# Two attention layers on one core: bias sums of the second projection at other steps and in other banks, the first biases split ahead of v, and products of constants in the prologue

## The chip, the core and the metric

The kernel runs on one core of one Trainium2 chip. The metric is the time of one execution on the device, in microseconds (us). All inputs, weights and results are float32 and lie in the device's memory; they are laid out on the host beforehand.

## The reference

The input x has shape 4 x 32 x 32 x 768 (4 images of 1024 tokens). Two attention layers follow each other, each as x = x + layer(group_norm(x)). Cut to what matters:

```python
# layer 0
q, k, v = heads(xn @ Wq + bq), heads(xn @ Wk + bk), heads(xn @ Wv + bv)   # 12 heads of 64
attn = q @ k.T / 8 + rel_bias_h(q)[..., None] + rel_bias_w(q)[..., None, :]
x = x + softmax(attn) @ v @ Wp + bp
# layer 1
q, k, v = split(xn @ w_qkv.T + b_qkv)
q, k, v = [layer_norm(dwconv3x3(t, w_pool)) * g + b for t in (q, k, v)]
attn = (q * scale) @ k.T + rel_h(q)[..., None] + rel_w(q)[..., None, :]
o = softmax(attn) @ v + q
x = x + o @ w_proj.T + b_proj
```

## The kernel before

**Stages, pairs and steps.** A stage is one image in one layer; there are eight, in the order (image 0, layer 0), (1, 0), (0, 1), (1, 1), (2, 0), (3, 0), (2, 1), (3, 1). Each stage has six pairs of heads, so there are 48 pairs. The attention of a pair (`attend`, L687) is written as 16 steps: two chunks of 512 queries, two groups of four key tiles for each chunk, and four steps for each group. A group issues the scores of its four key tiles (lines L748 and L750: the product of q and k, and the biases added by a second product), the exponentials on ACT (L755) and the running sums on DVE (L762, L764), then has two steps in which other work is put in, then issues the weighted sums (`av`, L770), then again has two steps for other work. Other work is put in by step number through `at(step, piece)` and the table `events`; steps below 0 make the prologue.

**Order.** The order on PE, DVE, ACT and POOL is the program's order (a manual schedule), so an instruction that waits holds up all that follows on its engine. SP, whose queue starts the loads and stores, is not in that list: its order is decided by the compiler's scheduler.

**PSUM banks.** The scores use a fixed pair of banks for the first and the fourth key tile and two places, `place_b` and `place_c`, for the second and the third. Between the scores those places serve the other work: `bank(name)` hands out the next of a list that is set anew after the scores and after `av` (`behind_av` is place_c, place_c, the small bank, place_b, place_b). `small_bank(name)` is a single bank of its own. It is also used by the means of the group norm (`gn_mean` L322, `gn_var` L331), by the softmax's sums (`z`, L712) and by some products of layer 0.

**Bias.** The relative positions of a pair are computed by `positions` (L575): small products `rel` into PSUM, copied by ACT into the tile `whole` (L595, L596). `split` (L601) rounds `whole` into `high` on ACT (L606), leaves the rest in `whole` on DVE (L607), and spreads both over the tile `bias` by eight DMAs on POOL's queue for each chunk of queries (L617). The bias products L750 read that tile. `plan` (L620) lists for each pair which piece stands at which of its steps; the first two pairs use the first list, in which the products of v (`plain_v`) come in two halves. Pair 0's pieces stand at steps -16 to -6, that is, in the prologue.

**Sums of weights.** Products are done in a form with seven products for eight, which needs sums of blocks of the weights. `mix_weights(u)` (L263) loads two blocks (`mix_a`, `mix_b`), yields, then forms five sums on DVE (L291) and stores them (L292). For layer 1's projection (u of 12, 13 and 14) it first multiplies the unmixed weights by the v norm's offset: six products of one column for each block, L281, into a `pbias` bank, which DVE adds to the projection's bias (L282). A table of (u, call, step) says at which step the loads are called and at which the sums are formed.

**Prologue.** `group_norm` of the first stage ends with `gn_mean`, `gn_var`, a few operations of one column on DVE and ACT (`rsqrt`), and six operations that normalize xn (L338). The products of q and k of pair 0 (`qkv`, issued by the helper `halves`, L131) wait for these. `halves` issues each product as two halves of 64 output columns.

Of the kernel before, what the change touches and what calls it, by code (L numbers as in the profile page):

```python
# [17 lines left out]
P = 128  # L18
# [27 lines left out]
def two_layers(ctx: ExitStack, tc: tile.TileContext, keep, x_in, wqkv, wproj, rels, windows, vrow, small, const, onehot, picks, out):  # L46
# [19 lines left out]
    nc = tc.nc  # L66
# [52 lines left out]
    def bank(name):  # L119

        place = turn.pop(0)
        turn.append(place)
        return place.single(name) if place else small_bank(name)

    def small_bank(name):
        return ps_small.tile([P, 512], F32, tag="small", name=name)
# [14 lines left out]
    cst = fixed.tile([P, NCONST], F32, tag="cst", name="cst")  # L141
    nc.sync.dma_start(cst, const)
    ident = cst[:, IDENT : IDENT + P]
# [6 lines left out]
    def rsqrt(v, n, name):  # L150

        ln = stat.tile([P, n], F32, tag=f"ln{n}", name=f"ln_{name}")
        nc.scalar.activation(ln, v, AF.Ln)
        r = stat.tile([P, n], F32, tag=f"r{n}", name=f"r_{name}")
        nc.scalar.activation(r, ln, AF.Exp, scale=-0.5)
        t = stat.tile([P, n], F32, tag=f"t{n}", name=f"t_{name}")
        nc.vector.tensor_mul(t, r, r)
        nc.vector.tensor_mul(t, t, v)
        nc.vector.tensor_scalar(t, t, -0.5, 1.5, ALU.mult, ALU.add)
        nc.vector.tensor_mul(r, r, t)  # L160
        return r


    stages = [(b0 + k, layer) for b0 in range(0, B, 2) for layer in range(2) for k in range(2)]
# [98 lines left out]
    def mix_weights(u):  # L263


        a = wp.tile([P, NC, P], F32, tag="wproj", name="mix_a")
        b = wp.tile([P, NC, P], F32, tag="wproj", name="mix_b")
        if u < PROJ_SUMS:
            (pa, sa), (pb, sb) = two(u, 0) if u < V_SUMS else two(2 * (u - V_SUMS), 2)
            nc.sync.dma_start(a, wqkv[0, pa, :, sa])  # L270
            nc.sync.dma_start(b, wqkv[0, pb, :, sb])
        else:
            layer, m = divmod(2 * (u - PROJ_SUMS), NC)
            for i, w in enumerate((a, b)):
                nc.sync.dma_start(w, wproj[layer, :, :, m + i, :].rearrange("h p q -> p h q"))
        yield
        for i, w in enumerate((a, b)):
            if u >= PROJ_SUMS and layer:
                ps = small_bank("pbias")
                for n in range(NC):  # L280
                    nc.tensor.matmul(ps[:, 0:1], w[:, n, :], col(LN + 5), start=(n == 0), stop=(n == NC - 1))  # L281
                nc.vector.tensor_tensor(pbias[:, m + i : m + i + 1], ps[:, 0:1], col(BIAS[1] + 18 + m + i), ALU.add)  # L282
        a1, a2, b1, b2 = a[:, :3, :], a[:, 3:, :], b[:, :3, :], b[:, 3:, :]
        for n, to, x, y, op in (
            (2, None, a1, b2, ALU.add), (4, None, b1, a1, ALU.subtract), (0, b1, b1, b2, ALU.add),
            (1, a1, a1, a2, ALU.add), (3, a2, a2, b2, ALU.subtract),
        ):
            if to is None:
                to = wp.tile([P, HALF], F32, tag="x", name="mix")
                to = to[:, : 3 * P].rearrange("p (n c) -> p n c", c=P)  # L290
            nc.vector.tensor_tensor(to, x, y, op)  # L291
            nc.sync.dma_start(mixed[u][:, n], to)  # L292
        mixed_there.add(u)
        yield
# [12 lines left out]
    def group_norm(stage):  # L307

        xn = xns[stage]
        st = stat.tile([P, NC * 2, 6], F32, tag="bn", name="bn", bufs=1)  # L310
        for n in range(NC):
            for h in range(2):
                nc.vector.bn_stats(st[:, 2 * n + h, :], xn[:, n, h * HALF : (h + 1) * HALF])
            if n in (1, 3):
                yield
        mv = stat.tile([P, 2], F32, tag="mv", name="mv")
        nc.vector.bn_aggr(mv, st.rearrange("p a b -> p (a b)"))
        yield
        yield
        group = cst[:, GROUP : GROUP + P]  # L320
        ps = small_bank("gn_mean")
        nc.tensor.matmul(ps[:, 0:1], group, mv[:, 0:1], start=True, stop=True)  # L322
        mean = stat.tile([P, 1], F32, tag="gmean", name="gmean")
        nc.vector.tensor_copy(mean, ps[:, 0:1])  # L324
        d = stat.tile([P, 1], F32, tag="gd", name="gd")
        nc.vector.tensor_sub(d, mv[:, 0:1], mean)
        nc.vector.scalar_tensor_tensor(d, d, d, mv[:, 1:2], ALU.mult, ALU.add)
        yield
        yield
        ps = small_bank("gn_var")  # L330
        nc.tensor.matmul(ps[:, 0:1], group, d, start=True, stop=True)  # L331
        v = stat.tile([P, 1], F32, tag="gv", name="gv")
        nc.vector.tensor_scalar(v, ps[:, 0:1], EPS, None, ALU.add)
        yield
        r = rsqrt(v, 1, "gn")
        yield
        for n in range(NC):
            nc.vector.tensor_scalar(xn[:, n, :], xn[:, n, :], mean, r, ALU.subtract, ALU.mult)  # L338
            if n % 2:
                yield  # L340
# [22 lines left out]
    class Pair:  # L363
# [256 lines left out]
        def plan(self):  # L620

            Q, K, V = 0, 1, 2
            if not self.layer and not in_sevens(self.i):
                return [
                    (0, lambda: self.plain(Q, 0)),
                    (2, lambda: self.plain(Q, 1)),
                    (4, lambda: self.plain(K, 0)),
                    (5, lambda: self.positions(0)),
                    (6, lambda: self.plain(K, 1)),
                    (7, lambda: self.positions(1)),  # L630
                    (8, lambda: self.plain_v(0)),
                    (10, lambda: self.split()),
                    (10, lambda: self.plain_v(1)),
                ]
            if not self.layer:
                pieces = [
                    (0, lambda: self.sevens(Q, False)),
                    (2, lambda: self.sevens(Q, True)),
                    (6, lambda: self.positions(0)),
                    (8, lambda: self.positions(1)),  # L640
                    (10, lambda: self.split()),
                ]
                if self.hp % 2 == 0:
                    pieces += [(8, lambda: self.sevens(V, False)), (10, lambda: self.sevens(V, True))]
                return [(r + shift(self.i), piece) for r, piece in pieces]

            pieces = [
                (-8, lambda: self.padded(Q, 0)),
                (-6, lambda: self.padded(Q, 1)),
                (-4, lambda: self.padded(K, 0)),  # L650
                (-2, lambda: self.padded(K, 1)),
                (2, lambda: self.padded(V, 0)),
                (4, lambda: self.padded(V, 1)),
                (3, lambda: self.centre(Q)),
                (5, lambda: self.squares(Q)),
                (7, lambda: self.norm(Q)),
                (8, lambda: self.centre(K)),
                (9, lambda: self.back(Q, 0)),
                (9, lambda: self.back(Q, 1)),
                (10, lambda: self.squares(K)),  # L660
                (10, lambda: self.positions(0)),
                (11, lambda: self.positions(1)),
                (12, lambda: self.norm(K)),
                (12, lambda: self.split()),
                (13, lambda: self.centre(V)),
                (14, lambda: self.back(K, 0)),
                (14, lambda: self.back(K, 1)),
                (14, lambda: self.squares(V)),
                (15, lambda: self.norm(V)),
            ]  # L670

            taps = (
                (Q, -4, (2, 2, 2, 2, 1)),
                (K, 2, (2, 2, 2, 2, 1)),
                (V, 8, (2, 2, 3, 2)),
            )
            for s, r, counts in taps:
                lo = 0
                for n in counts:
                    pieces.append((r, lambda s=s, lo=lo, n=n: self.taps(s, lo, lo + n)))  # L680
                    r, lo = r + 1, lo + n
            return pieces
# [233 lines left out]

    for u, call, step in (
        (2, 0, 5), (7, 6, 11), (3, 13, 18), (4, 22, 29), (8, 31, 38), (5, 40, 47), (0, 49, 55), (6, 57, 63), (1, 65, 71),
        (9, 72, 77), (10, 78, 83), (11, 84, 89), (12, 138, 143), (13, 145, 150), (14, 152, 157),
    ):  # L920
        mix = mix_weights(u)
        for at_step in (call, step):
            at(at_step, lambda mix=mix: next(mix))
# [348 lines left out]
```

## Time and profile before

| what | us |
|---|---|
| runs of the kernel before | 3919.93, 3915.82, 3917.45 |
| their median | 3917.45 |
| the profiled execution's own time | 3920.75 |
| its span, from the first to the last instruction | 3918.9 |
| PE busy | 3835.0 (98%) |
| DVE busy | 2673.5 (68%) |
| ACT busy | 1850.3 (47%) |
| mean granted clock of TensorE | 0.993 |

How to read it: 1.85 us of the profiled execution lie outside its span. PE is the matrix engine (TensorE), DVE the vector engine, ACT the scalar engine, POOL and SP start transfers here. A busy PE is not a PE at its peak: its clock can be granted at half (0.50) for a while, and a product then takes twice as long while the engine still counts as busy. PE's idle time and its time at half clock are therefore read separately, the first from the list of waits and the second from tables by stretches of time.

### The profile page before, as it was taken

To read this page: it belongs to the slowest core of one execution; us is meant where nothing else is said; L and a number is where in the kernel's file an instruction comes from. 1 tells how busy PE (TensorE), PEld (TensorE's weight loads), DVE (VectorE), ACT (ScalarE), POOL (GpSimd) and SP (SyncE) were. 2 spreads that over 40 slices of the span, in tenths; PEclk is the share of its full clock that TensorE was granted. 3 is DMA by queue.
4 is the path that set the end of the run, shared out by engine and by line. 5 is a ranking of instruction groups with operands and counts; after the bars stand their busy time and mean duration, and the time that the engine had idled before them with its cause. 6 is when DMAs were issued, how large, how long until landed. Compare 5 with 4: busy or idle time off the path is not lost.

```text
span 3918.9 us, 79880 instructions
## 1 busy us (share of the span) xinstructions
PE 3835.0 (98%) x34738; PEld 1726.2 (44%) x34738; DVE 2673.5 (68%) x3088; ACT 1850.3 (47%) x2741; POOL 411.7 (11%) x776
## 2 busy tenths in 40 slices
PE   7999999999999999999899999999999999999998
PEld 3535535534344444444444455355443444434442
DVE  2566454448789988799654554445686898878885
ACT  2455434445345553455533554254553555535551
POOL 0111000110000010000010010011100010000010
PEclk9999999999999999999999999999999999999999
DMA  4344452331331122311144222522115121142112
GB/s 147 102 120 120 127 163 61 94 83 38 105 100 39 39 60 83 115 45 39 41 118 135 56 73 64 167 63 75 42 52 155 35 56 43 39 118 57 36 47 95
DMA packets 184710, 318.11 MB, mean 81 GB/s; under 512 B 24352, under 2 KB 77472, under 8 KB 184352
## 3 DMA queue, kind: packets, MB, share of 16 engines
q1 hardware_dynamic: 122912, 212.19, 17.3%
q0 software_dynamic: 61440, 100.71, 11.2%
q8 instruction: 277, 4.54, 0.5%
q14 instruction: 81, 0.66, 0.1%
HBM read 172.23 MB, written 39.91 MB: 54 GB/s over the span
## 4 chain that ended last, share of the span: by engine, by line
PE 86%; DVE 11%; DMA 1%; issue 1%; ACT 1%; POOL 0%; DVEq 0%; SPq 0%; ACTq 0%
PE qkv L131 18%; PE s L748 15%; PE av L770 15%; PE m4m L131 4%; PE m3m L131 4%; PE m1m L131 4%; PE s L750 4%; DVE shared L532 3%; PE p3p L131 3%; DVE acc L764 3%; PE p1p L131 3%; PE p4p L131 3%; PE ln_c L131 3%; PE rel L590 3%; PE z L712 2%; PE m L131 2%
## 5 line engine op out<-in xcount | busy, mean ns | idle before, releaser
L755 ACT ACTIVATE e<-s 128x1024 f32<-128x1024 f32 x768 | 777.2, 1025 | 412.1 <-PE s L750 379.5
L764 DVE TENSOR_TENSOR acc<-acc,e 128x1024 f32<-128x1024 f32 x576 | 705.5, 1225 | 182.7 <-ACT e L755 132.2
L131 PE MATMUL qkv<-xn,wqkv_t 128*64 128x512 f32 x3648 | 815.8, 596 | 6.8 <-DVE gmean L324 4.1
L748 PE MATMUL s<-q,k 64*128 64x512 f32 x3072 | 817.1, 609 | 4.3 <-ACT e L755 3.5
L532 DVE SCALAR_TENSOR_TENSOR shared<-shared,sm 128x1056 f32<-128x1056 f32 x576 | 758.4, 1317 | 15.0
L750 PE MATMUL s<-bias,ones 64*128 64x512 f32 x1536 | 617.0, 796 | 10.9 <-DMA bias<-high 7.5
L770 PE MATMUL av<-e,vt 128*64 128x512 f32 x2624 | 595.0, 595 | 0.0
L617 POOL DMA_DIRECT2D bias<-high x384 | 203.6, 546 | 3237.8 <-ACT high L606 3003.6
L131 PEld LDWEIGHTS qkv<-xn,wqkv_t 128*64 128x64 f32 x3648 | 254.2, 137 | 491.5 <-issue 481.6
L515 ACT ACTIVATE shared<-qkv,sm 128x512 f32<-128x512 f32 (+1 forms) x288 | 129.3, 502 | 632.7 <-PE qkv L131 632.7
L748 PEld LDWEIGHTS s<-q,k 64*128 64x128 f32 x3072 | 283.2, 188 | 263.2 <-issue 216.8
L770 PEld LDWEIGHTS av<-e,vt 128*64 128x64 f32 x2624 | 185.6, 137 | 347.1 <-issue 322.0
L762 DVE TENSOR_TENSOR acc<-e 128x1024 f32<-128x1024 f32 x96 | 117.5, 1224 | 285.9 <-ACT e L755 280.1
L750 PEld LDWEIGHTS s<-bias,ones 64*128 64x128 f32 x1536 | 150.8, 189 | 199.2 <-issue 191.6
L617 POOL DMA_DIRECT2D bias<-whole x384 | 206.1, 558 | 106.6 <-DVE whole L607 97.0
L705 ACT COPY weighed<-av 128x512 f32<-128x512 f32 x96 | 56.4, 587 | 279.3 <-PE av L770 279.3
L131 PEld LDWEIGHTS ln_c<-cst,shared 128*64 128x64 f32 x2304 | 130.9, 137 | 48.5 <-issue 41.0
L590 PEld LDWEIGHTS rel<-q,rel 64*32 64x32 f32 x6144 | 111.7, 105 | 78.0 <-issue 58.7
L131 PE MATMUL ln_c<-cst,shared 128*64 128x128 f32 x2304 | 138.9, 273 | 6.4 <-DVE shared L532 5.7
L131 PE MATMUL m4m<-xn,wqkv_t 128*64 128x512 f32 x528 | 122.4, 599 | 4.0 <-issue 3.0
L400 DVE TENSOR_TENSOR shared<-shared,m3m 128x512 f32<-128x512 f32 x66 | 45.4, 687 | 118.3 <-PE m3m L131 118.2
L590 PE MATMUL rel<-q_t,rel 64*32 64x32 f32 x6144 | 123.3, 195 | 2.3 <-issue 2.3
(149 smaller groups left out, 4234.8 us busy)
## 6 DMA issues: line engine op xcount, KB each, us to landing
bias<-high POOLq DMA_DIRECT2D x384, 128.0 KB, 2.8
bias<-whole POOLq DMA_DIRECT2D x384, 128.0 KB, 3.0
wqkv_t<-in_wqkv SPq DMA_DIRECT2D x78, 384.0 KB, 3.1
wqkv_t<-mixed SPq DMA_DIRECT2D x66, 384.0 KB, 3.1
wproj_t<-mixed SPq DMA_DIRECT2D x48, 384.0 KB, 3.3
wqkv_t<-in_wqkv SPq DMA_DIRECT2D x66, 192.0 KB, 2.5
xn<-in_x SPq DMA_DIRECT2D x24, 512.0 KB, 7.8
x<-in_x SPq DMA_DIRECT2D x48, 256.0 KB, 3.1
```

The source lines that it names most:

```text
L131: nc.tensor.matmul(ps[lo : lo + D], a[:, lo : lo + D], b, start=start, stop=stop, **kw)
L515: nc.scalar.activation(self.pad[s][:, rows, there : there + src.shape[2]], src, AF.Identity, bias=col(self.column(s)))
L532: nc.vector.scalar_tensor_tensor(y, window, tap, y, ALU.mult, ALU.add)
L590: nc.tensor.matmul(ps[lo : lo + S, k * S : (k + 1) * S].rearrange("p (b c) -> p b c", b=2), rel[rows, 2 * self.layer + i, first : first + ...
L617: nc.gpsimd.dma_start(sets, some.unsqueeze(1).to_broadcast([D // 2, 2, QC]))
L712: nc.tensor.matmul(z[j * D : (j + 1) * D, :], cst[:, ONES : ONES + D], acc[:, j, :], start=True, stop=True,)
L748: nc.tensor.matmul(ps[:, j, :], k[rows, keys], q[rows, cols], start=True, stop=False)
L750: nc.tensor.matmul(ps[:, j, :], ones[rows, keys], bias[c][rows, kt // 2, :], start=False, stop=True,)
L755: nc.scalar.activation(e, ps, AF.Exp)
L762: nc.vector.tensor_tensor(acc, es[0], es[1], ALU.add)
L764: nc.vector.tensor_tensor(acc, acc, e, ALU.add)
L770: nc.tensor.matmul(av[j * D : (j + 1) * D, :], pair.vt[:, kt, j * D : (j + 1) * D], e[:, j, :], start=(kt == 0), stop=(kt == NKT - 1),)
```

## The change

It has three parts. The sums of layer 1's projection weights (u of 12, 13, 14) are called and formed at other steps: loads at 124, 137, 149 instead of 138, 145, 152, sums at 135, 147, 159 instead of 143, 150, 157, and their `pbias` products take their PSUM from `bank` instead of `small_bank`. In the plan of the first two pairs, `split` stands at the pair's step 8, ahead of both halves of v, instead of at step 10, between them. And in the first group norm five products of constants (the identity by 384 columns of the constants' tile) are issued after `gn_var`, into the small bank; nothing reads them.

```diff
@@ mix_weights
             if u >= PROJ_SUMS and layer:
-                ps = small_bank("pbias")
+                ps = bank("pbias")
                 for n in range(NC):
                     nc.tensor.matmul(ps[:, 0:1], w[:, n, :], col(LN + 5), start=(n == 0), stop=(n == NC - 1))
@@ group_norm
         nc.vector.tensor_scalar(v, ps[:, 0:1], EPS, None, ALU.add)
         yield
+        if stage == stages[0]:
+
+            ps = small_bank("warm")
+            for _ in range(5):
+                nc.tensor.matmul(ps[:, : 3 * P], ident, cst[:, : 3 * P], start=True, stop=True)
         r = rsqrt(v, 1, "gn")
@@ plan
                     (7, lambda: self.positions(1)),
+                    (8, lambda: self.split()),
                     (8, lambda: self.plain_v(0)),
-                    (10, lambda: self.split()),
                     (10, lambda: self.plain_v(1)),
@@ the table of (u, call, step)
-        (9, 72, 77), (10, 78, 83), (11, 84, 89), (12, 138, 143), (13, 145, 150), (14, 152, 157),
+        (9, 72, 77), (10, 78, 83), (11, 84, 89), (12, 124, 135), (13, 137, 147), (14, 149, 159),
```

## The prediction

> **What bounds the kernel now.** I read the page first, then PE's list of waits, then tables by stretches for the granted clock, then the timelines of the places that the change touches. The page's first part and its chain of waits say that PE sets the end:
>
> ```profile
> PE 3835.0 (98%) x34738; PEld 1726.2 (44%) x34738; DVE 2673.5 (68%) x3088; ACT 1850.3 (47%) x2741; POOL 411.7 (11%) x776
> PE 86%; DVE 11%; DMA 1%; issue 1%; ACT 1%; POOL 0%; DVEq 0%; SPq 0%; ACTq 0%
> ```
>
> So PE's own time counts, and its idle time counts, 84 us in all (3918.9 - 3835.0). The list of PE's waits (in total, times, longest) has four rows at the places of this change:
>
> ```profile
> PE s L750 <- DMA bias<-high: 7.5, 3, 4.3
> PE pbias L281 <- DVE pbias L282: 3.7, 3, 3.2
> PE qkv L131 <- DVE xn L338: 2.8, 1, 2.8
> PE pbias L281 <- DVE gmean L324: 2.0, 1, 2.0
> ```
>
> These are small. What follows them is not in the list: half clock. The table by stretches shows it (length, busy time and instructions of PE, PEld, DVE, ACT, POOL, then the clock):
>
> ```profile
> 61.99:65.40 3.41, 3.41 (x12) 2.04 (x10) 0.75 (x1) 1.86 (x2) 0.46 (x1) 0.50 0.51 112
> 703.70:713.94 10.24, 9.99 (x38) 7.33 (x39) 2.97 (x8) 1.44 (x2) 1.00 (x2) 0.50 0.54 163
> 751.48:754.90 3.42, 3.42 (x12) 1.39 (x10) 2.00 (x7) 2.89 (x5) 0.00 (x0) 0.50 0.67 238
> 792.44:799.27 6.83, 6.83 (x22) 3.76 (x24) 2.72 (x6) 0.00 (x0) 0.44 (x1) 0.50 0.67 198
> ```
>
> Each is a multiple of 3.41 us, and each begins after a stretch in which PE did little: the wait for the bias before 61.26, and the pbias products. Such a window costs about 1.7 us where PE has work. Seven of the run's further windows at 0.50 lie at other places (from 1871 on) and stay.
>
> **Part 1, the split ahead of v.** The timeline of the first scores (start, length, engine, operation, idle time before it):
>
> ```profile
> 50.70 0.59 ACT L473 COPY vt<-v 128x512 f32<-128x512 f32 x1 [3.78 <-PE v L131]
> 51.19 1.05 ACT L606 CAST high<-whole 128x1024 fp32r<-128x1024 f32 x1
> 52.54 2.23 POOL L617 DMA_DIRECT2D bias<-high  x4 [52.08 <-ACT high L606]
> 54.73 2.11 POOL L617 DMA_DIRECT2D bias<-whole  x4
> 55.83 1.13 PE L748 MATMUL s<-q,k 64*128 64x512 f32 x4
> 61.26 0.51 PE L750 MATMUL s<-bias,ones 64*128 64x512 f32 x2 [4.31 <-DMA bias<-high]
> ```
>
> ACT casts `high` only after its copy of v's first half, which ends v's products at 50.7, though `whole` was there at 46.92 (L596 at 45.90 lasts 1.02). With split first, the cast starts at 46.95, 4.24 earlier, and DVE (idle there for 29.36 us) and POOL follow with the same durations: POOL issues from 48.30 to 52.6, and the biases land 4.4 us after the last issue as before, at 57.0 at the latest, earlier if they meet less traffic (the load of wqkv at 55.94 ran into them). PE reaches L750 at 56.39 in the normal rhythm (0.56 after the scores' start, as at 80.52 and 81.08). So 0 to 0.6 us of wait is left; I take 0.3. Queued behind the cast on ACT are v's two copies; the first is ready at 50.70, when the cast has long ended (48.0). The block of scores takes 10.81 us (55.83 to the next product at 66.64) against 4.56 for an undisturbed one (80.52 to 85.08): 6.25, of which 4.9 is the wait and the rest the window at 62. Gain **6.0**. For pair 1 the same edit moves split from step 10 to 8: its scores come at step 16, POOL's second chunk waits for step 12 as before, and nothing behind it on POOL is needed sooner; 0.
>
> **Part 2, the bias sums.** First what does not move: the order on SP's queue is the same row for row in both builds. The loads of u = 12 were issued at 569.8 and 572.1, over 130 us ahead of their use at 703.4, those of 13 and 14 right behind the stores of the sums before them (712.6, 754.9). Calling them earlier is worth 0. The sums move on PE and DVE:
>
> ```profile
> 701.05 0.38 PE L322 MATMUL gn_mean<-mv,cst 128*128 128x1 f32 x2
> 703.44 2.51 PE L281 MATMUL pbias<-sm,mix_a 128*128 128x1 f32 x12 [2.00 <-DVE gmean L324]
> 706.20 2.72 PE L281 MATMUL pbias<-sm,mix_b 128*128 128x1 f32 x12 [0.25 <-DVE pbias L282]
> 787.69 1.50 PE L281 MATMUL pbias<-sm,mix_a 128*128 128x1 f32 x12
> 792.37 2.68 PE L281 MATMUL pbias<-sm,mix_b 128*128 128x1 f32 x12 [3.19 <-DVE pbias L282]
> 794.98 5.76 PE L770 MATMUL av<-e,shared 128*64 128x512 f32 x16
> ```
>
> All share the small bank, which DVE frees behind its running sums (at 703.3) and behind its normalizing of xn (at 792.3). What they take now, by starts on PE:
> - u = 12: 701.05 to the scores at 708.85 is 7.80; gn_mean alone would take 0.31 (as gn_var at 742.91). The scores then take 7.03 against 4.55. Sum 9.97.
> - u = 13: 746.80 to 749.98 is 3.18; the scores behind (751.20) take 6.24 against 4.55. Sum 4.87.
> - u = 14: 787.69 to 794.98 is 7.29; av takes 5.69 against 3.58. Sum 9.40.
>
> Together 24.2. At steps 135, 147 and 159 the 24 products of a u cost 24 x 0.107 (spacing in the warm rows) plus 0.2 for the change of form, 2.8 each, 8.4 in all. They get separate banks: place_c and the small one at 135, two singles of place_c at 147 and at 159. Their last readers are done: at 135 and 159 a copy or exponential of the group before, at 147 DVE's L434, 0.7 us of work beside a product of 2.58. So PE waits 0. Added is a wait of the third score pair (place_c) for the pbias addition: it comes 2.2 us after the scores' start; the addition comes by 684.2 against 687.5 at 135 (DVE's last piece before it ends at 683.3), by 741.2 against 743.3 at 147, by 794.2 against 796.4 at 159. The whole rest of the scores would queue behind it. DVE's five sums (0.55 each, 2.7) now stand ahead of the next group's running sums, whose first input comes 2.4 us after the scores' start, so 0.3 late on an engine that is 68% busy: 0. Without cooling the gain is 15.8.
>
> But products of one column cool the clock wherever they stand: the window 748.07 to 751.48, filled with pbias and rel products (3.1 us of low work), was followed by 0.50; the window from 758.31, with 2.1 to 2.5 us of it, was not. At 135 the rel products stand right ahead, 4.0 us of low work; at 147 and 159 it is 2.8. With a limit of about 2.6 us in one window, windows falling anywhere, that gives chances of some 0.65, 0.3 and 0.3, so one window, 1.7. [...] Gain **14.1**, between 5.6 (two windows at each place) and 15.8.
>
> **Part 3, products of constants.** They start at 16.85, when DVE has read gn_var (L333 ends at 16.76). PE's next work, qkv, starts at 19.34 and runs at half speed up to 24.47, though the clock column says 1.00 there: 10 products in 21.06 to 24.47 against 18 in the next window. No row shows a product of the full 128 x 128 form with many columns. From one side: a pair of halves does the same arithmetic, 0.853 us for 512 columns in the slow stretch, so 0.64 for 384 and 3.2 for five. qkv then starts at 20.3, 1.0 late, but the window up to 21.06 is full, the clock rises 3.41 earlier, and the first product, then held by DVE's xn (last ready at 22.9), ends at 23.45 instead of 24.47: 1.0 gained. [...] I take **0**, with 1.0 gained and 2 lost as ends.
>
> **Sum.** 6.0 + 14.1 + 0 = 20.1; 3920.75 - 20.1 = 3900.65. That is the profiled execution, which lies 3.3 above the median of the runs; I cannot tell whether its surplus is windows at these very places (then nothing is to be subtracted) or elsewhere, and take off half: **3899**.
>
> **Rivals.**
> - *The clock cools at every new place* (two windows for each u, also if pbias runs colder than its rows): gain 5.6 + 6.0 = 11.6, so 3909.2 less 1.6, 3907.5. For it: the three old places made six windows. Against: four of those six came with waits that go. Chance 0.15.
> - *The bias is late anyway.* Its 1 MB a chunk is served in its own time, and traffic, not the late issue, held it. For it: 4.4 us from last issue to L750, against a median of 2.8 to 3.0. Against: the load it met comes 3.4 us after the last issue now. Gain of part 1 near 0: 3905. Chance 0.08.
> - [...] Chance 0.5, whichever of the other cases holds, and inside the range of each.
> - *Slower: DVE gets late at the new steps.* The third score pair waits for the pbias addition behind DVE's running sums. It bites once DVE is over 2.0 (at 147) or 3.3 us behind; to lose more than 7.8 us, each place must cost (24.2 + 6.0 + 7.8) / 3 = 12.7, that is 2.8 own time, a wait of about 5 and three cold windows, DVE 7 to 8 us behind; from there on 3925.3 and more. At 690 to 700 it was busy 9.69 of 10, but PE never waited over 3.2 for it. Chance 0.04.
>
> **Numbers.** The forecast (3893 to 3906, up to two cold windows) has 0.73. A difference of 0.2%, 7.8 us, is about what a measurement of this kernel can tell from no change. Faster than 3909.6: all of the forecast and of the late bias, and half or more of the cooled clock, 0.90; same 0.06; slower 0.04. The range goes from all gains without a cold window (6.25 + 15.8 + 1.0, from the median's side: 3894.4, two more for windows elsewhere) to the cooled clock with part 3 lost: 3892 to 3911.
>
> **What the profile after would show.** L750 of the first scores starts 0.5 to 1 us after their L748, with no window at 0.50 behind it; the two pbias waits are gone from PE's list; gn_mean is followed by the scores within 0.4 us; blocks of scores behind pbias take 4.55, with at most one at 6.2; the products of constants last 3.2 or over 5 us, and which one is read off qkv's start, 20.3 or 22.2. The prediction is wrong if new waits stand at the third score pair behind pbias, or if the bias still lands over 1 us after PE asks for it.

## The result, and the profile after

| | median of runs | lowest to highest | profiled execution, its span |
|---|---|---|---|
| before | 3917.20 us (6 runs) | 3914.54 to 3919.93 | 3920.75, 3918.9 |
| changed | 3900.91 us (6 runs) | 3898.63 to 3902.24 | 3898.63, 3896.8 |

The ratio is 0.9958 (95% interval 0.9947 to 0.9969): 16.3 us less. The changed kernel's profile starts with the busy time of each engine, and its chain of waits still ends in PE:

```profile
PE 3826.2 (98%) x34748; PEld 1720.1 (44%) x34748; DVE 2674.1 (69%) x3088; ACT 1849.1 (47%) x2741; POOL 412.1 (11%) x776
PE 86%; DVE 11%; issue 1%; DMA 1%; ACT 1%; SPq 0%; POOL 0%; DVEq 0%
```

PE's busy time fell by 8.8 us and its idle time from 84 to 70.6 (3896.8 - 3826.2), although its first wait, for x, was 2.6 us longer. Products at half clock count as busy (3.41 of 3.41 us in the rows at 0.50 below), so the first of these numbers holds the windows that are gone, and the products that were added.

**The first scores (part 1).** In the timeline after (start, length, engine, operation, idle time before it) ACT casts `high` ahead of both copies of v, POOL has issued everything for the first chunk by 55.35, and the scores start 3.2 us after that:

```profile
49.71 1.05 ACT L611 CAST high<-whole 128x1024 fp32r<-128x1024 f32 x1
51.06 2.22 POOL L622 DMA_DIRECT2D bias<-high  x4 [50.60 <-ACT high L611]
53.24 2.11 POOL L622 DMA_DIRECT2D bias<-whole  x4
53.46 0.58 ACT L478 COPY vt<-v 128x512 f32<-128x512 f32 x1 [2.71 <-PE v L131]
58.58 1.13 PE L753 MATMUL s<-q,k 64*128 64x512 f32 x4
59.15 0.80 PE L755 MATMUL s<-bias,ones 64*128 64x512 f32 x2
```

L755 starts 0.57 us after L753, without a wait. The block takes 4.55 us (58.58 to 63.14) instead of 10.81.

**The bias sums (part 2).** The timeline of PE at the three places:

```profile
678.09 1.50 PE L281 MATMUL pbias<-sm,mix_a 128*128 128x1 f32 x12
679.45 1.48 PE L281 MATMUL pbias<-sm,mix_b 128*128 128x1 f32 x12
680.86 1.20 PE L753 MATMUL s<-q,k 64*128 64x512 f32 x4
...
728.48 1.50 PE L281 MATMUL pbias<-sm,mix_a 128*128 128x1 f32 x12
729.84 1.48 PE L281 MATMUL pbias<-sm,mix_b 128*128 128x1 f32 x12
731.25 1.13 PE L753 MATMUL s<-q,k 64*128 64x512 f32 x4
...
777.92 1.50 PE L281 MATMUL pbias<-sm,mix_a 128*128 128x1 f32 x12
779.28 1.48 PE L281 MATMUL pbias<-sm,mix_b 128*128 128x1 f32 x12
780.69 2.03 PE L753 MATMUL s<-q,k 64*128 64x512 f32 x4
```

No line has a wait. From the first product to the scores it is 2.77 us each time, against the 2.8 of the prediction. The first scores after the third place need 2.03 us for what takes 1.13 after the second: half clock. The table by stretches (length, busy time of PE, PEld, DVE, ACT, POOL, granted clock, DMA share, GB/s) has such a window behind two of the three places:

```profile
681.79:685.20 3.41, 3.41 (x12) 1.73 (x10) 1.89 (x4) 1.57 (x2) 0.00 (x0) 0.50 0.80 287
731.25:735.10 3.85, 3.85 (x25) 2.06 (x24) 3.68 (x7) 2.33 (x3) 0.00 (x0) 1.00 0.58 205
780.78:784.19 3.41, 3.41 (x12) 1.75 (x12) 2.72 (x6) 1.00 (x1) 0.00 (x0) 0.50 0.66 218
```

**The products of constants (part 3).** PE's timeline in the prologue:

```profile
17.30 0.59 PE L322 MATMUL gn_mean<-mv,cst 128*128 128x1 f32 x2 [17.30 <-DVE mv L317]
18.59 0.58 PE L331 MATMUL gn_var<-gd,cst 128*128 128x1 f32 x2 [0.70 <-DVE gd L327]
19.43 5.25 PE L339 MATMUL warm<-cst 128*128 128x384 f32 x10 [0.25 <-DVE gv L333]
24.61 1.94 PE L131 MATMUL qkv<-xn,wqkv_t 128*64 128x512 f32 x8
```

Everything here lies 2.6 us later than before, since x landed later in this execution. So distances count: from gn_mean to the first rel product it was 22.77 us before (14.69 to 37.46), and is 22.91 now.

**Two idle gaps.** Inside the products into the bank `m4m` (of the form with seven products for eight) two gaps have gone, which the prediction passed over. The list of PE's waits counts them with others in one row, first before, then after:

```profile
PE m4m L131 <- issue: 6.0, 6, 3.0
PE m4m L131 <- issue: 3.8, 3, 3.0
```

In the timeline before they read

```profile
615.16 1.42 PE L131 MATMUL m4m<-wqkv_t,xn 128*64 128x128 f32 x21
617.21 1.64 PE L131 MATMUL m4m<-wqkv_t,xn 128*64 128x128 f32 x26 [0.63 <-issue]
...
761.65 1.53 PE L131 MATMUL m4m<-wqkv_t,xn 128*64 128x128 f32 x24 [1.32 <-issue]
```

and after, the same 48 records run through (the profile has two records for a product here):

```profile
611.65 2.84 PE L131 MATMUL m4m<-wqkv_t,xn 128*64 128x128 f32 x48
```

"issue" means that PE waited for nothing that the profile shows. The groups with the gaps took 0.9 and 1.5 us longer than the same groups without.

### The profile page after: what moved, and what is told of

Read it like the earlier page. It is cut to its first block, busy times and chain, and to the rows that moved or that the text cites. A ratio compares the mean times of both kernels' runs of the same rounds, so it can differ in the third digit from the quotient of the medians.

```text
span 3896.8 us, 79900 instructions
## 1 busy us (share of the span) xinstructions
PE 3826.2 (98%) x34748; PEld 1720.1 (44%) x34748; DVE 2674.1 (69%) x3088; ACT 1849.1 (47%) x2741; POOL 412.1 (11%) x776
## 3 DMA queue, kind: packets, MB, share of 16 engines
q1 hardware_dynamic: 122912, 212.19, 17.3%
## 4 chain that ended last, share of the span: by engine, by line
PE 86%; DVE 11%; issue 1%; DMA 1%; ACT 1%; SPq 0%; POOL 0%; DVEq 0%
PE qkv L131 18%; PE s L753 15%; PE av L775 15%; PE m1m L131 4%; PE m3m L131 4%; PE m4m L131 4%; PE s L755 4%; DVE shared L537 3%; PE p3p L131 3%; DVE acc L769 3%; PE p1p L131 3%; PE p4p L131 3%; PE ln_c L131 3%; PE rel L595 3%; PE z L717 2%; PE m L131 2%
## 5 line engine op out<-in xcount | busy, mean ns | idle before, releaser
L753 PE MATMUL s<-q,k 64*128 64x512 f32 x3072 | 816.5, 608 | 4.7 <-ACT e L760 3.8
L755 PE MATMUL s<-bias,ones 64*128 64x512 f32 x1536 | 615.5, 794 | 4.7 <-DMA bias<-whole 2.5
L753 PEld LDWEIGHTS s<-q,k 64*128 64x128 f32 x3072 | 283.8, 188 | 260.8 <-issue 214.9
L755 PEld LDWEIGHTS s<-bias,ones 64*128 64x128 f32 x1536 | 150.2, 188 | 193.1 <-issue 188.0
```

What stands on the lines that cost most here:

```text
L753: nc.tensor.matmul(ps[:, j, :], k[rows, keys], q[rows, cols], start=True, stop=False)
L755: nc.tensor.matmul(ps[:, j, :], ones[rows, keys], bias[c][rows, kt // 2, :], start=False, stop=True,)
```

## The experiments

Kernels measured together ran on one chip with the kernel before, so each is given as a difference from the median of its runs there and as a ratio with its 95% interval. That median was 3919.0 us for the four kernels of the first section below; 3917.2 for the two halves of part 2, the one-column constants and the three products a block; and 3916.7 for the other four.

### The parts by themselves

Part 1 alone (only the line of `split` moved):

```diff
+                    (8, lambda: self.split()),
                     (8, lambda: self.plain_v(0)),
-                    (10, lambda: self.split()),
```

> The kernel before with part 1 alone (split ahead of v). My theory (bias ready when PE asks, so the 4.9 us wait and the half-clock window behind it both go): the first block of scores takes 4.55 us instead of 10.81, the run 6.3 us less than before (2.6 us less would be the wait without the window's share halved twice, so anything from 5.5 to 7 fits). Rival 1, the bias is late whatever the issue time: within 1 us of before. Rival 2, only the wait counts and the half clock costs nothing: 4.9 us less, with a window at 0.50 still behind the block. On the side: two idle gaps of PE inside products of m4m, 0.63 us at 617 and 1.32 us at 760 in the profile before, are gone in the profile after; if part 2 removed them they are still here, if they come and go from run to run they may be gone.

Measured: 3912.48, 6.5 us less, ratio 0.9981 (0.9972 to 0.9990). In its timeline the cast comes before the copies, and the scores wait for nothing:

```profile
48.18 1.05 ACT L606 CAST high<-whole 128x1024 fp32r<-128x1024 f32 x1
51.94 0.59 ACT L473 COPY vt<-v 128x512 f32<-128x512 f32 x1 [2.71 <-PE v L131]
57.06 1.13 PE L748 MATMUL s<-q,k 64*128 64x512 f32 x4
57.62 0.80 PE L750 MATMUL s<-bias,ones 64*128 64x512 f32 x2
```

The block takes 4.55 us, and no window at 0.50 follows. So the late issue held the bias, not the traffic, and 6.26 us of the block were wait and half clock. The two gaps inside m4m are still here (1.12 us at 611, 0.90 at 755).

Part 2 alone (the three steps, and `bank("pbias")`):

> The kernel before with part 2 alone (bias sums at steps 135, 147, 159, in a bank of their own turn). By the rows of the two profiles: before 24.2 us at the three places, after 3 x 2.77 of own time and two half-clock windows of 1.7, so 12.5 us less than before; with the two idle gaps inside m4m gone as well, 14.8. Theory of the missed term (the gaps belong to part 2): 14 to 15.5 less, no gap at 617 or 760. Rival (the gaps are chance): 12 to 13 less on the median.

Measured: 3906.10, 12.9 less, ratio 0.9965 (0.9952 to 0.9979). The gap at 617 is still here (1.19 us), and 0.28 us is left of the one at 760 (now at 753). My theory had both gaps go with part 2; that was wrong for the first of them.

Part 3 alone:

> The kernel before with part 3 alone (five products of constants). [...] Rival, the earlier clock helps: 1.0 us less, the block ends 21.8 us after gn_mean.

Measured: 3916.37, 2.6 less, ratio 0.9995 (0.9986 to 1.0004), which can't be told from no change. The distance from gn_mean to the first rel product is 23.36 us, 0.6 more than before; the rival's 21.8 did not come. Yet this execution is 3.7 us quicker than the one before between 573 and 878 us, where nothing was edited: both gaps inside m4m are gone, and one half-clock window fewer came (five, not six).

Parts 1 and 2 without 3:

> The changed kernel without the products of constants (parts 1 and 2). Theory (part 3 is worth nothing): as fast as the changed kernel, 16.3 us below before, within 0.7. Rival, part 3 carries 1 us of the gain: 15.3 below. Rival, part 3 costs up to 2 us: 17 to 18 below. If the parts are independent, this one's gain is the sum of those of the kernels with part 1 alone and part 2 alone.

Measured: 3901.74, 17.3 less, ratio 0.9956 (0.9942 to 0.9970), against 0.9958 with part 3. Part 3 is worth nothing that the time can tell. The gap inside m4m is back:

```profile
610.04 1.41 PE L131 MATMUL m4m<-wqkv_t,xn 128*64 128x128 f32 x21
612.40 1.64 PE L131 MATMUL m4m<-wqkv_t,xn 128*64 128x128 f32 x26 [0.95 <-issue]
```

It lies behind the 21st record of the group, as it did before. So it is tied to the program, not to chance.

### The two halves of part 2

> The kernel before with half of part 2: the bias sums at steps 135, 147 and 159, but still in the small bank. Theory 1 (the place counts, the bank little): 12 to 13 us less than before, as the kernel with all of part 2 (12.9 less). Rival (the bank counts: the second block of six products waits in the small bank for DVE's addition of the first, behind DVE's running sums): waits of 1 to 3 us at L281 in each of the three places, 4 to 10 us less than before.

Measured, new steps and small bank: 3911.66, 5.6 less, ratio 0.9986 (0.9977 to 0.9996). Each second block waits for DVE's addition of the first, and one place waits for L434, which reads the small bank as well:

```profile
734.35 1.50 PE L281 MATMUL pbias<-sm,mix_a 128*128 128x1 f32 x12 [0.79 <-DVE shared L434]
736.10 1.70 PE L281 MATMUL pbias<-sm,mix_b 128*128 128x1 f32 x12 [0.25 <-DVE pbias L282]
```

The waits are 0.25 us each, not the 1 to 3 of the rival. But they stretch the slow work of a place from 2.77 to 3.2 to 3.6 us, and all three places are followed by half clock, four windows in all.

> The kernel before with the other half of part 2: banks in turn, at the old steps 143, 150 and 157. Theory 1 (the place counts): the waits of 2.0 and 3.2 us stay or go, but the products still stand next to rel and gn products, so at least four of the six half-clock windows of the old places stay, and the gain is 2 to 7 us. Rival (the bank is all): 12 to 13 us less than before.

Measured, old steps and banks in turn: 3903.63, 13.6 less, ratio 0.9971 (0.9962 to 0.9981), as much as with both halves. My first theory falls: it is the bank. At the old place of u = 12, where PE had waited 2.00 us, the timeline is now

```profile
702.65 0.38 PE L322 MATMUL gn_mean<-mv,cst 128*128 128x1 f32 x2
702.89 1.48 PE L281 MATMUL pbias<-sm,mix_a 128*128 128x1 f32 x12
704.23 1.48 PE L281 MATMUL pbias<-sm,mix_b 128*128 128x1 f32 x12
705.64 1.84 PE L748 MATMUL s<-q,k 64*128 64x512 f32 x4
```

with 2.75, 2.77 and 2.77 us at the three places, and two windows instead of six. A one-word edit has the gain; with it, the steps and the calls ahead of time add nothing that the time can tell.

### Gaps that move with the number of instructions

```diff
-                nc.tensor.matmul(ps[:, : 3 * P], ident, cst[:, : 3 * P], start=True, stop=True)
+                nc.tensor.matmul(ps[:, 0:1], ident, cst[:, 0:1], start=True, stop=True)
```

> The changed kernel with its five products of constants cut from 384 columns to one (the same number of instructions on PE, about 0.5 us of work). It tests why PE's idle gap inside m4m (0.6 to 1.2 us at 610 to 617, in all kernels without part 3 so far) is gone in both kernels with part 3. [...] Rival (the earlier clock, or chance): the gap of 0.9 to 1.2 us is back. Time within 1.5 us of the kernel without the products (17.3 us below before) either way.

Measured: 3898.78, 18.4 less, ratio 0.9958 (0.9944 to 0.9971). The gap stays away with products of one column, which take 2.29 us in place of 5.25. That fits instructions that arrive in blocks, and the profile page's table of DMA queues shows such blocks (packets, MB, share of 16 engines):

```profile
q8 instruction: 277, 4.54, 0.5%
```

These are 16384 bytes each, one for every 251 records of products and weights on PE (2 x 34738 / 277). The trace gives their start times. In the six kernels without products of constants one starts 0.03 to 0.16 us before the m4m group, and PE goes on 2.2 to 2.7 us after that start in all six: 609.96 and 612.40 in the kernel with parts 1 and 2. In the eight kernels with products in the prologue it starts 1.3 to 2.0 us before the group, that is before the 128 records of rel (256 with their weights) have rushed through PE in 1.2 us, and there is no gap. The gaps of the later group, near 750, agree: PE goes on 2.2 to 2.6 us after a block's start there too. Two kernels that hold the products of constants still have that later gap, of 0.8 and 0.6 us (the two with three products a block): their blocks start 0.23 and 0.09 us before the group. A late start is not enough for a gap, however: in the kernel with one product a block the start is 0.26 us before the later group, and PE does not wait.

To test what sets the start, 64 products of 64 x 32 took the place of the five. With two records of a product and two of weights each, they are 256 records, about one block by the 251 above:

```diff
-            for _ in range(5):
-                nc.tensor.matmul(ps[:, : 3 * P], ident, cst[:, : 3 * P], start=True, stop=True)
+            for _ in range(64):
+                nc.tensor.matmul(ps[:S, :S], cst[:D, :S], cst[:D, :S], start=True, stop=True)
```

> [...] Rival (any work in the prologue takes the gap away, or chance): no gap.

Measured in a single run: 3903.49, and no gap:

```profile
615.04 2.84 PE L131 MATMUL m4m<-wqkv_t,xn 128*64 128x128 f32 x48
```

If the start went by the place in the stream modulo a block, the gap should have come back. So this simple form of the theory falls, as far as 256 records are one block, which is the author's estimate from the 251. That PE waits for a block of instructions there is supported by the times, but no run moved a block and nothing else. Why the block is asked for 1.3 us and more earlier as soon as anything stands in the prologue stays open. (The time of this kernel goes to its prologue: its 64 products take 7.0 us, and rel comes 27.2 us after gn_mean.)

### Less one-column work

The bias sums need not read the raw weights: `a1` and `b1` hold a1 + a2 and b1 + b2 after the additions of `mix_weights`, and the vector is the same for all six slices. So three products do for six, one call later (sums at steps 131, 143, 155, products at 135, 147, 159 as in the changed kernel). Cut to the added lines; the loop over six slices goes:

```diff
         mixed_there.add(u)
         yield
+        for i, w in enumerate((a1, b1)):
+            ps = bank("pbias")
+            for n in range(NC // 2):
+                nc.tensor.matmul(ps[:, 0:1], w[:, n, :], col(LN + 5), start=(n == 0), stop=(n == NC // 2 - 1))
+            nc.vector.tensor_tensor(pbias[:, m + i : m + i + 1], ps[:, 0:1], col(BIAS[1] + 18 + m + i), ALU.add)
+        yield
```

> The changed kernel with each pbias taken from sums that the kernel makes anyway (a1 + a2 and b1 + b2 hold the sum over the six slices in three), so 3 products a block instead of 6; sums at steps 131, 143 and 155, the products four steps later, where the changed kernel has them. Theory (own time 2.8 and a half-clock window of 1.7 at two of the three places, and the window comes from over 2.6 us of one-column work in it): own time 1.5 a place, no window at steps 147 and 159, perhaps one at 135 next to rel: 5 to 7.5 us less than the changed kernel, 21.5 to 24 less than before. Rival 1, the windows cool anyway: 4 less than the changed kernel. Rival 2, DVE's sums four steps earlier make the running sums late: no gain, waits of PE for acc or e.

Measured: 3891.31, 25.9 less, a little more than the 21.5 to 24 expected; ratio 0.9939 (0.9926 to 0.9953). Own time is 1.43 us a place, and no window at 0.50 came at any of them, not even next to the rel products at 135:

```profile
677.97 0.83 PE L292 MATMUL pbias<-sm,mix_a 128*128 128x1 f32 x6
678.66 0.81 PE L292 MATMUL pbias<-sm,mix_b 128*128 128x1 f32 x6
```

The table by stretches has clock 1.00 around that place:

```profile
676.00:690.00 14.00, 14.00 (x318) 7.47 (x316) 8.32 (x12) 11.00 (x15) 0.00 (x0) 1.00 0.21 59
```

The same amount of work as in the changed kernel, but spread (a `yield` between the two blocks, four steps apart):

> The changed kernel with all 72 pbias products, but the two blocks of a u four steps apart (127 and 131, 143 and 147, 159 and 163), none next to rel products. Theory (a window cools when about 2.6 us of one-column work or pause fall into one window of 3.41 us): no window at 0.50 between 640 and 830, the six blocks cost 1.4 each and the scores behind them 4.55: 2.5 to 4 us less than the changed kernel. Rival (the amount of one-column work near by counts, or the phase): one to three windows stay, within 1.5 us of the changed kernel.

Measured: 3895.51, 21.2 less, ratio 0.9944 (0.9929 to 0.9959). The time alone does not separate it from the changed kernel (the intervals overlap), but its rows do: six blocks of 1.41 to 1.43 us, and clock 1.00 in the stretches of all of them (two blocks lie in the first):

```profile
640.00:670.00 30.00, 30.00 (x149) 11.35 (x145) 12.66 (x17) 11.62 (x16) 2.43 (x5) 1.00 0.23 64
720.00:740.00 20.00, 20.00 (x226) 9.18 (x224) 9.66 (x14) 8.68 (x11) 0.00 (x0) 1.00 0.41 129
765.00:780.00 15.00, 15.00 (x118) 8.72 (x116) 7.88 (x9) 6.50 (x8) 4.82 (x8) 1.00 0.57 137
```

So it is the concentration of such work that counts here, not its amount: 2.77 us in one piece was followed by 0.50 at two of the changed kernel's three places, 1.41 to 1.43 us at none of these six.

Three products a block, and one-column products of constants:

> The kernel with three products from the ready sums for each pbias, and now the five products of constants cut to one column. In ten profiles so far the first rel product came 21.8 to 22.9 us after gn_mean without products of constants (six kernels), 22.9 to 24.1 with the full ones (three), 21.3 with one-column ones (one). Theory (the full ones hold PE past the point where xn is ready): 1 to 2.5 us less than with the full ones, so 27 to 28.5 less than before, rel 21.3 to 22.3 after gn_mean. Rival (that was the phase of the clock's windows): within 0.7 of the kernel with the full ones, 25.9 less than before.

Measured: 3892.64, 24.1 less, ratio 0.9936 (0.9923 to 0.9950): not told apart by time from the kernel with the full ones, and short of the 27 to 28.5 expected. Rel comes 22.53 us after gn_mean, against 24.05 there; the expected 21.3 to 22.3 was missed by a little.

One product a block, DVE adding the three slices, again with the one-column constants. Cut, and shown against the kernel with three products; its loop over three slices becomes one product:

```diff
+        if u >= PROJ_SUMS and layer:
+            both = [stat.tile([P, P], F32, tag=f"both{i}", name="both", bufs=1) for i in range(2)]
+            for to, w in zip(both, (a1, b1)):
+                nc.vector.tensor_tensor(to, w[:, 0, :], w[:, 1, :], ALU.add)
+                nc.vector.tensor_tensor(to, to, w[:, 2, :], ALU.add)
         yield
-        for i, w in enumerate((a1, b1)):
+        for i, w in enumerate(both):
```

> The same, with the three slices of each sum added up by DVE (four additions of 128 columns more for each u) and one product a block. Theory: own time of a place 0.4 instead of 1.43 us, 3 us less than the kernel with three products and one-column constants, no half-clock window at the three places: 30 less than before. Rival 1, DVE (68 percent busy) gets late by its additions and PE waits for e or acc behind them: 0 to 2 us less or even more. Rival 2, the wait of PE for the sum.

Measured: 3886.64, 30.1 less, ratio 0.9929 (0.9915 to 0.9942), the lowest of all. The two products of a place are one line now, and take 0.54 us:

```profile
676.44 0.61 PE L296 MATMUL pbias<-sm,both 128*128 128x1 f32 x4
```

Of the blocks of scores behind the three places one took 4.91 us instead of 4.55 (at 770.57) and one 4.65; no half-clock window came. The time is 6.0 us below that of the kernel with three products and one-column constants, where 3 was expected; the stretch of the next section gives 3.3 of it (24.6 less 21.3).

## Why the prediction was right, and where it was not

The forecast of 3899 stood 1.9 us below the median. Its parts fared differently, and that the total came so near is in part luck: a cooling taken too small and two gaps not counted at all nearly cancel. For the sums, the stretch from the 113th to the 177th exponential holds the three places and both gaps; before it took 304.1 us (573.47 to 877.55). What a profile is quicker there is made up as follows (us; half clock is what the block behind a place takes over its usual time):

| kernel | own time of the three places | half clock behind them | idle gaps in m4m | quicker than before |
|---|---|---|---|---|
| new steps, small bank | 10.9 | 6.0 | 1.0 | 8.2 |
| old steps, banks in turn | 8.3 | 3.4 | 1.5 | 13.0 |
| part 2 alone | 8.4 | 3.2 | 1.5 | 13.0 |
| parts 1 and 2 | 8.4 | 4.9 | 1.0 | 11.9 |
| changed kernel | 8.3 | 3.4 | 0 | 14.8 |
| one-column constants | 8.3 | 5.1 | 0 | 13.1 |
| three products a block | 4.3 | 0 | 0.8 | 21.1 |
| the same, one-column constants | 4.3 | 0 | 0.6 | 21.3 |
| spread | 8.6 | 0 | 0 | 18.2 |
| one product a block | 1.6 | 0.5 (no window) | 0 | 24.6 |
| shifted by 256 instructions | 8.3 | 3.4 | 0 | 14.6 |

Taking the three middle columns from 26.6 (the prediction's 24.2 for the old places, and 2.4 by which the two gaps lengthened their groups) gives the last one within 0.5 us in every row. So the 24.2 stands.

- **Part 1: right.** 6.0 was predicted, the block shows 6.26 and the kernel with this part alone 6.5. The 0.3 us of wait that the prediction left was not there. The rival of the late bias falls.
- **Part 2, own time and waits: right.** 2.77 a place for 2.8, no wait of PE for its bank, and no wait of the third score pair for the addition. That earlier calls are worth nothing fits the kernel with the old calls. What the prediction left together, steps and bank, comes apart: the bank has the gain.
- **Part 2, the cooling: mis-sized.** The term was one window, 1.7 us, by a limit of 2.6 us of low work in one window, an estimate between the 2.5 and the 3.1 us of two windows before. In the five kernels with the unspread products at the new steps and banks in turn (changed, part 2 alone, parts 1 and 2, one-column constants, shifted) 12 of 15 places cooled, one window each: four at 135, three at 147, five at 159. That is 2.4 windows a kernel, some 4.1 us. The rival with two windows at each place, 3907.5, did not come either.
- **Why the limit was too high.** It came from counting rel products as low work. The traces show where the windows lie: in each execution all of them start on one grid (before, from 61.99 to 3864.44, 1114 times 3.4133 us), whose offset differs between executions (0.55 us before, 2.53 after). So one can count, for every window, the time from the start of each one-column product to PE's next product, waits included. Between 560 and 870 us of all 14 profiles, each of the 25 windows at full clock with 1.91 us of it or more was followed by 0.50, and none with 1.81 or less was. Rel products beside it did not bring half clock about. Two windows of the kernel shifted by 256 instructions, each with the one behind it, show both: the first has 1.72 us of pbias and 1.22 of rel, the second 2.03 of pbias and no rel.

```profile
679.78:683.20 3.42, 3.42 (x148) 2.90 (x144) 2.60 (x6) 2.17 (x3) 0.00 (x0) 1.00 0.02 5
683.20:686.61 3.41, 3.41 (x24) 2.40 (x26) 2.19 (x6) 0.97 (x1) 0.00 (x0) 1.00 0.22 78
...
730.98:734.40 3.42, 3.42 (x27) 2.90 (x29) 1.48 (x6) 0.72 (x1) 0.00 (x0) 1.00 0.37 115
734.40:737.81 3.41, 3.41 (x12) 1.39 (x8) 2.98 (x5) 2.05 (x2) 0.00 (x0) 0.50 0.82 291
```

The prediction's window from 748.07, with its 3.1 us, held 1.91 of pbias and their wait; the rest was rel. So products of one column did not cool the clock at every place. Which of the 15 places cooled is the offset's doing: 2.77 us can be cut by a window's edge into pieces too short to cool (1.72 and 1.05 in the first window above and the next), 1.43 us stays under the 1.81 however it falls.

- **A term missed: the gaps.** The prediction sorted idle time by named waits, and passed over the rows that end in "issue". 2.4 us of the profile's gain come from two of these. In the changed kernel's profile they more than make up for the one window by which the cooling was under-sized there, 2.4 against 1.7.
- **Part 3: 0 was taken, with 1.0 gained and 2 lost as ends, and only a loss was real.** No run shows the 2 us; what the runs showed in their place is a loss of 0.8 on the mean, as counted below. Five products take 5.2 to 6.4 us: 6.4 from +2.12 us after gn_mean in the kernel with three products a block, where the clock rose only at +8.01, so 1.28 each at half clock. The 3.2 us, from which the 1.0 was worked out, misread the rows before. The first 512 columns of q are six slices in two halves, 12 products, and the 36 products of three such chunks are 72 records, so two for each half and four for a pair. At half clock two records start every 0.853 us (0.43 from 24.49 on):

```profile
19.34 18.18 PE L131 MATMUL qkv<-xn,wqkv_t 128*64 128x512 f32 x72 [2.78 <-DVE xn L338]
20.25 0.24 PEld L131 LDWEIGHTS qkv<-xn,wqkv_t 128*64 128x64 f32 x2 [0.61 <-DVE xn L338]
21.11 0.24 PEld L131 LDWEIGHTS qkv<-xn,wqkv_t 128*64 128x64 f32 x2 [0.62 <-issue]
21.96 0.24 PEld L131 LDWEIGHTS qkv<-xn,wqkv_t 128*64 128x64 f32 x2 [0.62 <-DVE xn L338]
```

So a pair of halves takes 1.71 us for 512 columns, not 0.853, and 1.28 for 384, as the full form. The rows before held the price, and the two forms cost the same. From gn_mean to the first rel it was 21.8 to 22.9 us in six kernels without these products, mean 22.5, and 22.9, 23.0, 23.4 and 24.1 in four with them: 0.8 lost on the mean, inside the named ends. The marks "over 5 us" and "qkv starts at 22.2" were the author's estimate; the run gave 5.25 us, and 5.2 from the first product of constants to qkv (19.43 to 24.61), where the mark has 5.35 (16.85 to 22.2).

- **The half of the profile's surplus: not settled.** The profiled executions differ by 22.1 us, the medians by 16.3. Of the 22.1, 18.3 had come by the 177th exponential. Another 3.3 come in the last 160 us, where nothing was edited and where the execution before has a half-clock window (3864.44 to 3867.85) that the one after lacks. That speaks for a surplus elsewhere than at the three places, but it is one pair of executions.

## What to carry to other kernels

Small products that share one bank with a busy reader cost three times in this kernel: the wait (2.00 us at the first place before, 3.19 at the third), the half clock that followed the wait (10.24 and 6.83 us there), and the half clock behind the low work itself (3.41 us after 2.77 us of such products without a wait). Give them a bank in turn first, then make them fewer (sums that exist already, additions on an engine with room) or spread them, before moving them in the order; in this kernel a block of 1.43 us never cooled. On a kernel bound by TensorE, read the granted clock behind each low stretch and the idle rows that end in "issue" as terms of the sum (here 1.7 us for a window and 2.4 for two gaps), since a list of named waits shows neither. A warm-up has to end when its successor's input is ready (here qkv started 7.31 us after gn_mean with it, 4.65 before): price it from the rows, and first count how many records of the profile make one product.

## What the runs showed of the hardware

- The clock cooled while PE counted as fully busy: 2.77 us of one-column products without an idle gap were followed by 3.41 us at 0.50 in 12 of 15 places, 1.43 us in none of 12. The window ahead of the first of these in the profile after (678.38 to 681.79) has PE busy for 3.41 of 3.41 us. What went with it was how much of the low work fell into one window of 3.41 us: between 560 and 870 us of the 14 profiles, with 1.91 us or more, waits between the products included, the next window was at 0.50 in 25 of 25 cases, with 1.81 or less in none.
- Instruction packets of 16384 bytes arrived by DMA, 277 in the profile before, one for every 251 records on PE. Where one started only 0.03 to 0.16 us before the group that follows the 128 records of rel, PE stood still for 0.6 to 1.2 us, in six kernels at the same group, and five products (20 instructions) some 590 us earlier removed it there.
- A full 128 x 128 float32 product of 384 columns took 1.28 us at half clock; a pair of 64-column halves took 1.71 for 512 columns, which is the same for each column.
